# A mixture-of-experts kernel: expert rows fetched in 32-channel pieces and turned by VectorE in 32x32 squares

## The chip, the cores and the metric

The kernel runs on one core of a Trainium2 chip. The metric is the device time of one execution in microseconds. A core has five engines with queues of their own: PE (matrix multiply), DVE (VectorE), ACT (ScalarE), POOL (GpSimd) and SP (which issues most DMAs here). Engines wait for each other and for DMAs through semaphores. The profile calls PE's loading of a stationary operand PEld; it lies beside the multiplications.

## What is computed

Two layers over 2708 nodes with 256 channels. Layer 0 is a graph attention, then a causal self-attention with a mixture of experts; layer 1 is a second graph attention and a second mixture of experts. Only the mixture of experts is touched. Cut from the reference (layer 0; layer 1 has no `ln2_w`):

```python
flat = _rmsnorm(x, ln2_w).reshape(-1, Cx)
probs = jax.nn.softmax(flat @ router_w.T, axis=-1)
tp, ti = jax.lax.top_k(probs, TOPK)                       # 2 of 8 experts
tp = tp / (jnp.sum(tp, axis=-1, keepdims=True) + 1e-09)
weights = jnp.sum(tp[..., None] * jax.nn.one_hot(ti, NE, dtype=flat.dtype), axis=1)
for e in range(NE):
    hh = jax.nn.silu(flat @ w1[e].T) * (flat @ w3[e].T)   # 256 -> 682
    out = out + weights[:, e:e + 1] * (hh @ w2[e].T)      # 682 -> 256
```

Everything is in float32.

## The kernel before

The router sends each node's row, twice, into a DRAM buffer `xs`: expert `e` owns the rows from `e * CAP` on, filled from the front. A row of `xs` has 268 floats (1072 bytes): 256 channels, the node's number, eight expert weights, and filling.

Each expert has five fixed blocks of 128 rows. Some are computed already before the stage (three in layer 0, four in layer 1), and the last two of expert 7 in layer 0 later. What an expert needs beyond five blocks is done in half blocks of 64 rows of any expert, two halves at a time. `experts_blocks` (L2011) runs the rest. It makes a list `units`: for each expert its left blocks in pairs, a single one where the number is odd, and ahead of each of the experts 2 to 5 a unit of two half blocks, whose experts are read from a table at run time (`e` is None there). Both layers have 25 units. Experts 2 to 5 have a cycle of four units: halves, pair, pair, single.

For each unit:

- `fetch` (L2037) has SP load the rows of its blocks, 128 rows x 1072 bytes each (L2049, halves at L2045), into slots of `XR`, a ring of 17 slots. A slot is free again when the rows computed from it have been added to the output, since it holds the node numbers by which the addition is addressed.
- `front` (L2057) brings the channels onto the partitions: two TensorE transposes per block (L2063) of 128x128 into a PSUM tile `pt`, then ACT copies it to `xT` in SBUF (L2065 in layer 1). In layer 0 it does so in two activations which also multiply by `ln2_w` (L2068).
- `up` (L2072) has PE multiply by w1 and w3 in six groups of hidden channels (L2085), in five PSUM banks `pup` by turns; ACT applies silu (L2089), DVE the product (L2090, L2093), which gives `hT`. Half blocks go through `up_halves` (L2116 and after).
- `down` (L2096) has PE multiply by w2 (L2100), DVE weigh the rows (L2103), and POOL add them to the output in DRAM by node number (`add_rows`, L621). Half blocks: `down_halves`, L2150.

In iteration `k` of the main loop, the code issues weight loads, `fetch` of unit `k + 5` (`AHEAD`), `up` of unit `k`, `front` of unit `k + 2`, and `down` of unit `k - 1`. So on PE the transposes of unit `k + 2` stand between `up` of `k` and `down` of `k - 1`. The framework then orders each engine's instructions by their dependencies and its own estimates, so that SP's fetches and loads come in another order than they stand in the code.

Expert weights (2.1 MB an expert, six DMAs each, L2004 to L2009) go by turns into three rooms (`arena` twice, `room`), two experts ahead. The half blocks' two experts go into two further rooms, `more`, which are free again after the last product of the former halves (L2150).

Of the kernel before, what the change touches and what calls it, by code (L numbers as in the profile page):

```python
# [10 lines left out]
F32 = mybir.dt.float32  # L11
AF = mybir.ActivationFunctionType
# [8 lines left out]
P = 128  # L21
N = 2708
C = 256
KC = C // P
# [13 lines left out]
GI = 6  # L38
NB = 5
HALF_B = 64  # L40
AHEAD = 5
MORE = 8
LEAST, MOST = 512, 960
# [6 lines left out]
CAP = (NT + 1) * P  # L50
# [12 lines left out]
V_C1, V_C2, V_SS, V_SD, V_B1, V_LN1, V_LN2 = range(0, 14, 2)  # L63
# [86 lines left out]
def adj_ffn_kernel(ctx, tc, x, adj, vecs, bias_rows, tab, w_gnn0, w_gnn1, wqkv, wo,  # L150
                   r0, r1, w1_0, w3_0, w2_0, w1_1, w3_1, w2_1, out):
    nc = tc.nc
# [27 lines left out]
    vec = const.tile([P, 14], F32, name="vec")  # L180
# [434 lines left out]
    def add_rows(acc, ys, tokens, layer, e=None):  # L615

        i = nc.gpsimd.indirect_dma_start(  # L621
            out=acc[:, :], out_offset=bass.IndirectOffsetOnAxis(ap=tokens.bitcast(I32), axis=0),
            in_=ys, in_offset=None, compute_op=ALU.add,
            **(dict(bounds_check=N - 1, oob_is_err=False) if layer else {}))
        now, past = added.setdefault(acc.name, [[], []])
        if now and now[0][0] != (e, layer) or e is None:
            past[:], now[:] = now, []
        for _, name in past:
            tc.add_manual_dep(i.ins, name, NEEDS, reason="may add to the same rows")
        now.append(((e, layer), i.ins.name))  # L630
        if e is not None:
            key = f"{acc.name}_{layer}_{e}"
            tc.declare_no_dep(i.ins, group=key, reason="other tokens")
            tc.add_to_no_dep_group(key, i.ins)
# [1201 lines left out]
    def after_all(i, xs):  # L1836
        for name in written[xs.name]:
            tc.add_manual_dep(i.ins, name, NEEDS, reason="reads what they wrote")
# [132 lines left out]
    def clear(xs, e):  # L1971

        at, n = e * CAP + LEAST, MOST + HALF_B - LEAST
        nc.sync.dma_start(out=xs[at:at + n, :].rearrange("(b p) c -> p b c", p=P),
# [17 lines left out]
    def load_expert(room, w1, w3, w2, e, used=False):  # L1992
        cut = NF * P
        a, b, c, d = weights_at(room)
        if not used:
            nc.gpsimd.memset(c, 0.0)
            nc.gpsimd.memset(d[:, NF, :], 0.0)
        if isinstance(e, int):
            w1v, w3v = (w[:, e, :].rearrange("(k p) h -> p k h", p=P) for w in (w1, w3))
            w2v = w2[e]  # L2000
        else:
            w1v, w3v = (w[:, bass.ds(e, 1), :].rearrange("(k p) o h -> p k (o h)", p=P) for w in (w1, w3))
            w2v = w2[bass.ds(e, 1)].rearrange("o h c -> (o h) c")
        nc.sync.dma_start(out=a, in_=w1v[:, :, :cut])  # L2004
        nc.sync.dma_start(out=b, in_=w3v[:, :, :cut])
        nc.sync.dma_start(out=c[:, :, :REST], in_=w3v[:, :, cut:])
        nc.sync.dma_start(out=c[:, :, HIGH:], in_=w1v[:, :, cut:])
        nc.sync.dma_start(out=d[:, :NF, :], in_=w2v[:cut, :].rearrange("(k p) c -> p k c", p=P))
        nc.sync.dma_start(out=d[:REST, NF, :], in_=w2v[cut:, :])  # L2009

    def experts_blocks(layer, w1, w3, w2, xs, acc, arena):  # L2011
# [8 lines left out]
        with ExitStack() as s:  # L2020
            sp = s.enter_context(tc.tile_pool(name=f"slot{layer}", bufs=2))
# [6 lines left out]

            ring = [XR[:, t, :] for t in range(AHEAD, NT)]

            with tc.tile_pool(name=f"bpu{layer}", bufs=5, space=PSUM) as pu, \
# [4 lines left out]

                def fetch(unit):  # L2037
                    xts = []
                    for e, j in unit:
                        xt = ring.pop(0)  # L2040
                        ring.append(xt)
                        if e is None:
                            for h in range(2):
                                row = register(tab[0:1, 1, j + h:j + h + 1], NE * CAP - HALF_B)
                                after_all(nc.sync.dma_start(out=xt[h * HALF_B:(h + 1) * HALF_B, :],  # L2045
                                                            in_=xs[bass.ds(row, HALF_B), :]), xs)
                        else:
                            row = e * CAP + j * P
                            after_all(nc.sync.dma_start(out=xt, in_=xs[row:row + P, :]), xs)  # L2049
                        xts.append(xt)  # L2050
                    return xts

                def register(of, top):
                    return nc.values_load(of, engines=[SP], min_val=0, max_val=top,
                                          skip_runtime_bounds_check_because="the table is clamped")

                def front(xts):  # L2057
                    B = len(xts)
                    pt = pt_.tile([P, KC, 2, P], F32, tag="tr", name="pt")
                    xT = sp.tile([P, KC, 2, P], F32, tag="xT", name="xTs", bufs=3)  # L2060
                    for b, xt in enumerate(xts):
                        for c in range(KC):
                            nc.tensor.transpose(pt[:, c, b, :], xt[:, c * P:(c + 1) * P], ident)  # L2063
                    if layer == 1:
                        nc.scalar.copy(xT[:, :, :B, :], pt[:, :, :B, :])  # L2065
                    else:
                        for c in range(KC):
                            nc.scalar.activation(xT[:, c, :B, :], pt[:, c, :B, :], AF.Copy,  # L2068
                                                 scale=vec[:, V_LN2 + c:V_LN2 + c + 1])
                    return xT  # L2070

                def up(k, w, xT, B, between):  # L2072

                    hT = hTs[k % len(hTs)]
                    for n in range(NHC):
                        if n == NHC // 2:
                            between()
                        pp = pu.tile([P, 2, 2, P], F32, tag="pp", name="pup")
                        if n < NF:
                            parts = [(w[i][:, :, n * P:(n + 1) * P], P) for i in range(2)]  # L2080
                        else:
                            parts = [(w[2], HIGH + REST)]
                        for i, (wn, to) in enumerate(parts):
                            for c in range(KC):
                                nc.tensor.matmul(pp[:to, i, :B, :], wn[:, c, :], xT[:, c, :B, :],  # L2085
                                                 start=(c == 0), stop=(c == KC - 1))
                        sl = sp.tile([P, 2, P], F32, tag="sl", name="sl", bufs=3)
                        if n < NF:
                            nc.scalar.activation(sl[:, :B, :], pp[:, 0, :B, :], AF.Silu)  # L2089
                            nc.vector.tensor_tensor(hT[:, n, :B, :], sl[:, :B, :], pp[:, 1, :B, :], ALU.mult)  # L2090
                        else:
                            nc.scalar.activation(sl[:REST, :B, :], pp[HIGH:HIGH + REST, 0, :B, :], AF.Silu)
                            nc.vector.tensor_tensor(hT[:REST, n, :B, :], sl[:REST, :B, :], pp[:REST, 0, :B, :], ALU.mult)  # L2093
                    return hT
# [10 lines left out]

                halves = [slice(h * HALF_B, (h + 1) * HALF_B) for h in range(2)]

# [38 lines left out]
                def down_halves(w, hT, xt, gk):  # L2146
# [7 lines left out]
                    upper = sp.tile([P, 1], F32, tag="upper", name="upper")  # L2154
                    nc.vector.tensor_copy(upper[:HALF_B].bitcast(I32), xt[halves[1], C:C + 1].bitcast(I32))
                    add_rows(acc, yw[halves[0]], xt[:HALF_B, C:C + 1], layer)
# [44 lines left out]
                units = []  # L2201
                for e in range(NE):
                    left = [(e, j) for j in range(NB) if (e, j) not in done]
                    if 2 <= e < 2 + MORE // 2:
                        units.append([(None, 2 * (e - 2))])
                    units += [left[i:i + 2] for i in range(0, len(left), 2)]
                xt = [fetch(u) for u in units[:3]]
                nxt = [front(x) for x in xt[:2]]
                asked, more_asked = 1, 0
                waiting, downs = [], {}  # L2210
                for k, unit in enumerate(units):
                    e = unit[0][0]
                    if k == 1:
                        table()
                        xt += [fetch(u) for u in units[3:AHEAD + 1]]

# [5 lines left out]
                    if k == 0 or e is not None and e + 2 < NE and asked < e + 2 and units[k - 1][0][0] == e:  # L2222
                        asked += 1
                        load_expert(rooms[asked % 3], w1, w3, w2, asked, asked > 2)
                    if k and k + AHEAD < len(units):
                        xt.append(fetch(units[k + AHEAD]))
                    if unit[0] == (2, 2):
# [24 lines left out]
                    if k + 2 < len(units):  # L2252
                        nxt.append(front(xt[k + 2]))
# [159 lines left out]
```

## Time and profile before

| | us |
|---|---|
| median of 3 runs | 1482.06 |
| lowest and highest run | 1481.34, 1487.33 |
| the profiled execution | 1481.93 |
| its span, first to last instruction | 1479.8 |
| PE busy in the span | 1401.3 (95%) |
| DVE busy | 754.4 (51%) |
| ACT busy | 564.5 (38%) |
| POOL busy | 525.7 (36%) |

The span in 40 slices of 37 us, busy share in tenths (9 is 90% or more):

```profile
PE   6878999999999999999999899999999999999995
DVE  5688999975676322222222474767665322222221
ACT  2577866755544322222221454444333211222220
DMA  7689767440001476575212770624412867553111
```

The expert stage of layer 0 runs from about 503 us to 812 us (slices 14 to 22), that of layer 1 from about 1154 us to the end (slices 32 to 40). There PE is full and the other engines are mostly idle. The DMA row is the mean share of the 16 DMA engines. A busy PE alone doesn't say that PE sets the end; the chain of waits, followed back from the last instruction, does.

### The profile page before, as it was taken

The numbers are of one execution on the slowest core, as the hardware profiler recorded it, in microseconds if no ns is written. First come the engines' busy times: TensorE is split into PE (matmuls) and PEld (weight loads), VectorE is DVE, ScalarE is ACT, GpSimd is POOL, SyncE is SP. The second block draws the span as 40 slices with busy tenths as digits, with TensorE's granted clock in tenths as the row PEclk, the third lists the DMA queues.
The fourth block names the chain that finished last, engine by engine and source line by source line (L and its number), as shares of the span: only waits on it lengthen the run. The fifth ranks groups of instructions, "written<-read, shape, count | busy, mean of one in ns | idle before, by whom it ended". The sixth has DMA issues, their size and how long they took to land.

```text
span 1479.8 us, 20690 instructions
## 1 busy us (share of the span) xinstructions
PE 1401.3 (95%) x7344; PEld 1021.5 (69%) x7344; DVE 754.4 (51%) x1629; ACT 564.5 (38%) x1123; POOL 525.7 (36%) x677
## 2 busy tenths in 40 slices
PE   6878999999999999999999899999999999999995
PEld 5633433433334887888888878888768878888885
DVE  5688999975676322222222474767665322222221
ACT  2577866755544322222221454444333211222220
POOL 5677668773243312222222210031434212222222
PEclk9999999999999999999999999999999999999998
DMA  7689767440001476575212770624412867553111
GB/s 265 199 296 288 241 208 236 139 146 15 8 30 50 126 218 194 141 195 158 37 16 26 167 154 1 139 66 115 132 58 57 265 171 196 157 161 88 19 18 21
DMA packets 190679, 193.03 MB, mean 130 GB/s; under 512 B 90568, under 2 KB 162728, under 8 KB 187856
## 3 DMA queue, kind: packets, MB, share of 16 engines
q1 hardware_dynamic: 166262, 162.30, 35.5%
q0 software_dynamic: 20032, 25.71, 9.7%
q10 hardware_dynamic: 4270, 3.58, 0.7%
q8 instruction: 60, 0.98, 0.3%
q14 instruction: 55, 0.45, 0.1%
HBM read 119.81 MB, written 56.11 MB: 119 GB/s over the span
## 4 chain that ended last, share of the span: by engine, by line
PE 77%; DVE 8%; DMA 6%; POOL 4%; issue 2%; ACT 2%; another core or an unknown queue 0%; POOLq 0%; DVEq 0%; SPq 0%; ACTq 0%
PE pup L2085 23%; PE po L1602 14%; PE y L2100 12%; PE o L1146 5%; PE stt L1120 4%; DMA X<-hd,ix 3%; PE up L561 3%; PE pup L2116 3%; PE y L2150 1%; DVE es L1165 1%; DVE yT L1203 1%; PE pt L2063 1%; PE pm L1221 1%; PE po L948 1%; PE pt L584 1%
## 5 line engine op out<-in xcount | busy, mean ns | idle before, releaser
L2085 PE MATMUL pup<-xTs,arena 128*128 128x256 f32 (+2 forms) x1320 | 252.3, 350 | 0.6 <-ACT xTs L2068 0.6
L2085 PEld LDWEIGHTS pup<-xTs,arena 128*128 128x128 f32 (+1 forms) x1320 | 219.8, 190 | 27.7 <-PE y L2150 1.5
L1602 PE MATMUL po<-hb,PT 128*128 128x257 f32 (+2 forms) x968 | 226.0, 387 | 2.6 <-DVE PT L1595 2.6
L2089 ACT ACTIVATE sl<-pup 128x256 f32<-128x256 f32 (+1 forms) x210 | 73.7, 351 | 375.1 <-PE pup L2085 354.2
L1602 PEld LDWEIGHTS po<-hb,PT 128*128 128x128 f32 (+2 forms) x968 | 175.9, 188 | 41.6 <-issue 12.7
L2090 DVE TENSOR_TENSOR hT<-sl,pup 128x256 f32<-128x256 f32 (+1 forms) x210 | 79.6, 380 | 228.5 <-ACT sl L2089 228.3
L1126 ACT ACTIVATE e<-stt 128x1024 f32<-128x1024 f32 (+1 forms) x132 | 125.6, 986 | 93.0 <-PE stt L1120 63.8
L621 POOL DMA_INDIRECT out<-ys,XR x44 | 68.0, 1546 | 237.2 <-DVE ys L2103 169.2
L1165 DVE TENSOR_TENSOR es<-es,e 128x1024 f32<-128x1024 f32 x104 | 136.1, 1309 | 29.9 <-ACT e L1126 22.0
L621 POOL DMA_INDIRECT acc<-ys,XR x44 | 68.4, 1554 | 225.1 <-DVE ys L2103 153.7
L2100 PE MATMUL y<-arena,hT 128*128 128x256 f32 x612 | 136.7, 379 | 0.0
L1120 PE MATMUL stt<-qT,kT 64*128 64x512 f32 (+1 forms) x528 | 132.4, 611 | 4.3 <-ACT e L1126 3.9
L1829 POOL DMA_INDIRECT xs<-XR,place x88 | 93.3, 1061 | 91.7 <-DVE mk L1589 39.6
L1146 PE MATMUL o<-e,V 128*64 128x512 f32 (+1 forms) x528 | 124.3, 594 | 0.0
L2100 PEld LDWEIGHTS y<-arena,hT 128*128 128x128 f32 x612 | 114.3, 190 | 14.5
L1580 ACT ACTIVATE E<-sb,dcol 128x768 f32<-128x768 f32 (+1 forms) x88 | 75.3, 859 | 110.2 <-DVE PT L1595 106.7
L2103 DVE TENSOR_SCALAR ys<-y,XR 128x256 f32<-128x256 f32 x71 | 34.3, 484 | 146.6 <-PE y L2100 146.4
L2085 PE MATMUL pup<-xTs,room 128*128 128x256 f32 (+3 forms) x528 | 99.9, 346 | 0.0
L1120 PEld LDWEIGHTS stt<-qT,kT 64*128 64x128 f32 x528 | 44.4, 187 | 76.5 <-issue 62.3
L2085 PEld LDWEIGHTS pup<-xTs,room 128*128 128x128 f32 (+1 forms) x528 | 85.4, 189 | 9.8 <-PE y L2150 0.8
L1146 PEld LDWEIGHTS o<-e,V 128*64 128x64 f32 x528 | 33.0, 138 | 70.6 <-issue 55.6
L994 DVE MAX8 tops<-arena 128x8 f32<-128x2708 f32 (+1 forms) x22 | 65.3, 2970 | 0.3 <-DMA arena<-in_adj 0.3
(316 smaller groups left out, 1992.4 us busy)
## 6 DMA issues: line engine op xcount, KB each, us to landing
more<-in_w SPq DMA_DIRECT2D x48, 640.0 KB
arena<-in_adj SPq DMA_DIRECT2D x21, 1354.0 KB
arena<-in_w SPq DMA_DIRECT2D x36, 640.0 KB
mb<-mb SPq DMA_DIRECT2D x44, 352.0 KB
XR<-xs SPq DMA_DIRECT2D x80, 134.0 KB
xs<-none SPq DMA_DIRECT2D x16, 536.0 KB
room<-in_w SPq DMA_DIRECT2D x12, 640.0 KB
acc<-X SPq DMA_DIRECT2D x21, 128.0 KB
```

Of the source, the lines that this page charges most:

```text
L621: i = nc.gpsimd.indirect_dma_start(out=acc[:, :], out_offset=bass.IndirectOffsetOnAxis(ap=tokens.bitcast(I32), axis=0), in_=ys, in_offset= ...
L1120: nc.tensor.matmul(st[:r, g, c0(sb):], kT[a:b, sb * P:sb * P + r], qT[a:b, t0 + (sb == t0 + 1):t0 + 2, :, :], start=True, stop=True)
L1126: nc.scalar.activation(e[:r, :, c0(sb):], v[sb, "st"][:r, :, c0(sb):], AF.Exp, scale=1.0 / HD ** 0.5)
L1146: nc.tensor.matmul(v["o"][g * HD:(g + 1) * HD, c:], V[:r, sb, g * HD:(g + 1) * HD], v[sb][:r, g, c:], start=(n + i == 0), stop=(n + i == t ...
L1165: nc.vector.tensor_tensor(es, es, v[sb][:r, :, c:], ALU.add)
L1580: nc.scalar.activation(e[:q, :n], sb[:q, i0:i1], AF.Exp, bias=dcol[:q, j:j + 1], scale=SLOPE - 1.0)
L1602: nc.tensor.matmul(v["po", i][:r, :F], v["PT", j][:q, a:a + r], hb[:q, j, :], start=(j == 0), stop=(j == NT - 1))
L1829: i = nc.gpsimd.indirect_dma_start(out=xs[:, :], out_offset=bass.IndirectOffsetOnAxis(ap=at, axis=0), in_=src, in_offset=None)
L2085: nc.tensor.matmul(pp[:to, i, :B, :], wn[:, c, :], xT[:, c, :B, :], start=(c == 0), stop=(c == KC - 1))
L2089: nc.scalar.activation(sl[:, :B, :], pp[:, 0, :B, :], AF.Silu)
L2090: nc.vector.tensor_tensor(hT[:, n, :B, :], sl[:, :B, :], pp[:, 1, :B, :], ALU.mult)
L2100: nc.tensor.matmul(y, hT[:, n, b, :], w[3][:, n, :], start=(n == 0), stop=(n == NHC - 1))
```

## The change

For the pair and single units of fixed blocks, other than the first two of each layer (`in_pieces`), the 256 channels are no longer loaded as rows. SP loads only the last 12 floats of each row into the ring slot, and the channels in eight DMAs into a new tile `pieces`: each takes 32 channels of all rows of the unit and puts row `32 s + j` on partition `j` of one quarter of 32 partitions, at place `s`. So each of its runs is 32 floats, 128 bytes, and a pair has 256 runs in each DMA. There are five such tiles (`AHEAD`), each free again once it is turned. `front` then has DVE transpose all 32x32 squares within the tile, straight into `xT`: one instruction for a pair (128 x 512), two for a single block (128 x 128 each). In layer 0 ACT multiplies `xT` by `ln2_w` in place. Half-block units and the first two units keep the TensorE transposes. What is computed is the same.

```diff
+SQ = 32
 def fetch(unit):
     xts = []
+    in_pieces = unit[0][0] is not None and unit not in units[:2]
...
             row = e * CAP + j * P
-            after_all(nc.sync.dma_start(out=xt, in_=xs[row:row + P, :]), xs)
+            c0 = C if in_pieces else 0
+            after_all(nc.sync.dma_start(out=xt[:, c0:], in_=xs[row:row + P, c0:]), xs)
         xts.append(xt)
+    if in_pieces:
+        (e, j), B = unit[0], len(unit)
+        row = e * CAP + j * P
+        pieces = sp.tile([P, KC, 2, P], F32, tag="xp", name="pieces", bufs=AHEAD)
+        for k in range(KC):
+            for a in range(P // SQ):
+                c0 = k * P + a * SQ
+                after_all(nc.sync.dma_start(
+                    out=pieces[a * SQ:(a + 1) * SQ, k, :B, :].rearrange("j b (s i) -> j (b s) i", i=SQ),
+                    in_=xs[row:row + B * P, c0:c0 + SQ].rearrange("(s j) i -> j s i", j=SQ)), xs)
+        turned.append(pieces)
+    else:
+        turned.append(None)
     return xts
...
 def front(xts):
     B = len(xts)
+    xT = sp.tile([P, KC, 2, P], F32, tag="xT", name="xTs", bufs=3)
+    pieces = turned.pop(0)
+    if pieces is not None:
+        if B == 2:
+            nc.vector.transpose(xT.rearrange("p k b c -> p (k b c)"), pieces.rearrange("p k b c -> p (k b c)"))
+        else:
+            for c in range(KC):
+                nc.vector.transpose(xT[:, c, 0, :], pieces[:, c, 0, :])
+        if layer == 0:
+            for c in range(KC):
+                nc.scalar.activation(xT[:, c, :B, :], xT[:, c, :B, :], AF.Copy,
+                                     scale=vec[:, V_LN2 + c:V_LN2 + c + 1])
+        return xT
     pt = pt_.tile([P, KC, 2, P], F32, tag="tr", name="pt")
-    xT = sp.tile([P, KC, 2, P], F32, tag="xT", name="xTs", bufs=3)
     for b, xt in enumerate(xts):
         for c in range(KC):
             nc.tensor.transpose(pt[:, c, b, :], xt[:, c * P:(c + 1) * P], ident)
```

More of the change, by code (lines that the diff above doesn't have):

```diff
@@ L2055, in register @@
                                           skip_runtime_bounds_check_because="the table is clamped")
+                turned = []
                 def front(xts):
                     B = len(xts)
+                    xT = sp.tile([P, KC, 2, P], F32, tag="xT", name="xTs", bufs=3)
[11 more added lines that the diff above has]
+                        return xT
                     pt = pt_.tile([P, KC, 2, P], F32, tag="tr", name="pt")
-                    xT = sp.tile([P, KC, 2, P], F32, tag="xT", name="xTs", bufs=3)
                     for b, xt in enumerate(xts):
```

## The prediction

> **What bounds the kernel now.** I read the page first, then the two expert stages alone (the busy time in stretches 500 to 830 us and 1150 to 1480 us), then the chain of waits inside one expert, then the groups and SP's issues there.
>
> The stretches, with columns for the time and busy time of PE, PE's weight loads, DVE, ACT and POOL, then the granted clock, the DMA share and GB/s:
>
> ```profile
> 500.00:830.00 330.00, 325.61 (x1866) 277.64 (x1865) 83.25 (x242) 72.81 (x204) 75.23 (x62) 0.99 0.51 132
> 1150.00:1480.00 330.00, 313.13 (x1745) 265.29 (x1744) 80.09 (x242) 63.70 (x169) 70.41 (x51) 0.98 0.47 123
> ```
>
> PE is busy 98.7% and 94.9% of these stretches, DVE 25% and 24%, ACT 22% and 19%, the DMA engines about half. A busy PE is not yet a PE that ends last, so the chain of waits is what I rely on (start, length, what):
>
> ```profile
> 630.10 9.69 PE pup L2085 x44
> 639.79 0.22 PE pt L2063 x2
> 640.01 5.18 PE y L2100 x24
> 645.20 4.90 PE pup L2085 x44
> 650.10 0.44 PE pt L2063 x4
> 650.53 5.18 PE y L2100 x24
> 655.72 4.82 PE pup L2116 x40
> 660.54 0.59 PE pt L2063 x4
> 661.13 2.59 PE y L2100 x12
> ```
>
> It is PE work end to end. The transposes of `front` (L2063) stand in it with their whole length: two of them put 0.22 us between `up` and `down`, four 0.44 us, so 0.109 us each. The 0.59 us after the half-width products of L2116 holds 0.15 us more. The groups give each transpose a longer time, because a matmul's record includes its latency; the step in the chain is what counts:
>
> ```profile
> L2063 PE MATMUL pt<-ident,XR 128*128 128x128 f32 x158 | 27.0, 282 | 3.1 <-DMA XR<-xs 2.3 <-ACT xTs L2065 0.8
> L2068 ACT ACTIVATE xTs<-pt,vec 128x256 f32<-128x256 f32 (+1 forms) x50 | 18.6, 424 | 18.5 <-PE pt L2063 18.1
> L2065 ACT COPY xTs<-pt 128x512 f32<-128x512 f32 (+1 forms) x25 | 12.5, 501 | 13.8 <-PE pt L2063 9.2 <-DMA XR<-xs 4.2
> L2090 DVE TENSOR_TENSOR hT<-sl,pup 128x256 f32<-128x256 f32 (+1 forms) x210 | 79.6, 380 | 228.5 <-ACT sl L2089 228.3
> ```
>
> DVE waits 228 us for ACT at L2090 alone, ACT 354 us for PE at L2089: neither is the bound. SP is ahead of the work: it stops at row fetches until an old row slot has been added to the output, which is 17 blocks back in the ring:
>
> ```profile
> SPq L2049 <- DMA acc<-ys,XR: 86.5, 16, 12.4
> SPq L2049 <- DMA out<-ys,XR: 80.0, 17, 12.6
> ```
>
> **What the Trainium skill says.** "VectorE: DVE Perf Modes", section "The three transpose paths", gives VectorE 311 ns for a 128x128 bf16 transpose in 32x32 blocks and says that only such blocks are turned. The trace has no such instruction; as a size for it, L2090's 380 ns (shapes mixed) for mostly 256 f32 columns is of the same order. The same section warns that a copy which transposes by strides is 19 times slower when the innermost stride is large. Here the innermost run is 32 floats, contiguous at both ends, so I don't apply the factor. "DMA: Bandwidth & Descriptors", section "Why small descriptors are slow (HBM only)", names a fixed cost per packet and per descriptor. The trace agrees that small packets are poor in GB/s, and it has a near relative, the leftover weight columns (L2006 and L2007: 256 runs of 168 bytes each). In two quarter-microsecond stretches where these runs dominate:
>
> ```profile
> DMA packets 270, 0.06 MB, mean 235 GB/s; under 512 B 263, under 2 KB 263, under 8 KB 270
> q1 hardware_dynamic: 270, 0.06, 113.5%
> ...
> DMA packets 154, 0.02 MB, mean 95 GB/s; under 512 B 154, under 2 KB 154, under 8 KB 154
> q1 hardware_dynamic: 154, 0.02, 55.8%
> ```
>
> The share counts 16 engines, 4 engine-us in a quarter: 1.135 x 4 / 270 = 16.8 ns and 0.558 x 4 / 154 = 14.5 ns a packet. I take 15 ns for one of 128 bytes, bounds 10 and 30 (a read across a boundary, rows 1072 bytes apart).
>
> **The change, part by part.** A unit is one or two blocks of 128 rows. Each layer has 25 units, of which four are half-expert units and two are the first two; these six keep the old way. That leaves 19 units with 31 blocks in layer 0 and 19 with 32 in layer 1: 25 pairs and 13 singles, 63 blocks.
>
> *Removed from PE:* 63 x 2 = 126 of the 158 transposes, 126 x 0.109 = 13.7 us, all on the chain. If the extra 0.15 us after L2116 goes too (four places in layer 0 and three in layer 1), that is 1.0 us more. I take it as staying with whatever PE does next, since the switch from half-width products remains.
>
> *Added on DVE:* 25 turns of 128x512 and 26 of 128x128. From L2090 and the skill's 311 ns I estimate 0.3 us for the small one and 0.7 us for the large: 25 x 0.7 + 26 x 0.3 = 25 us in both layers together, bounds 20 and 60. DVE has 497 us free in the two stretches. In DVE's compiled order a turn stands among the hT products of the unit two before its own, and while it waits or runs, those products queue behind it. PE feels that only when all five `pup` banks are full. A group of a pair takes 9.50 / 6 = 1.6 us, so about 8 us are covered. A large turn of even 2 us leaves nothing visible. Without that cover each pair would lose its 0.7 us, 17 us in all.
>
> *ACT:* in layer 0 the scaling stays, now in place from SBUF and behind a turn; 38 activations of about 0.42 us become 38 of the same size. In layer 1, 19 copies of 0.5 us go, off the chain. Nothing counted: the up products need xT two units later, over 15 us.
>
> *DMA engines:* 63 x 1024 = 64,512 packets of 128 bytes at 15 ns are 968 engine-us, plus 8,064 row tails of 48 bytes at 13 ns, 105; less 8,064 row packets of 1072 bytes at about 55 ns (fitted over the stages' windows without software DMAs), 444. Net 629 engine-us, over 16 engines 39 us, spread over some 540 us. The share rises from about 0.5 to 0.57. Nothing on the chain.
>
> *SP:* each of the 38 units gains eight DMAs. L2006 with its 256 runs issues in 0.37 to 0.42 us, and a row fetch of L2049 in 0.36, so the issue time doesn't follow the run count. 38 x 8 x 0.45 = 137 us over both layers. In the compiled program each hardware DMA also waits for the one eight places before it, so eight are in flight at most. With 3 us each, that allows one per 0.4 us, about the issue time. In a steady expert of 46.7 us SP goes from 25 DMAs to 49. Weights that used to slip between row fetches now follow them. For expert 4, the pieces buffers (five) let its two pair fetches go at once, the half-expert weights still wait for L2150 at 582.5 us, and expert 4's own follow at about 590, ahead of the 603 us of before and of the need at 664.
>
> The tightest place is the start of layer 1: fifteen piece and tail DMAs come ahead of the half-expert weights, whose last issue was at 1176.9 us. 15 x 0.45 moves this to 1183.7, landing at about 1187 to 1188; PE wants them at 1195. Covered by 7 us; pieces of 1 us each would use it up.
>
> *Sum:* 13.7 us saved, and I allow 0.7 us for small waits at the two starts, where DMA is already 80% busy (507 to 553 us). The profiled execution took 1481.93 us (its span 1479.8), so 1481.9 - 13.0 = **1468.9 us**. The median of the three runs is 1482.06, 0.1 us off, so I use the number for it too.
>
> **Rivals.** *Part of the gain is given back (1478 us).* Late pieces at the start of a layer, or the turn standing in DVE's queue, hold PE for 4 to 5 us in each layer: 1468.9 + 2 x 4.5. For it: DMA is full there and weights are bunched with pieces. Against: the slack of 7 us above, and in layer 0 the half-expert weights are wanted only at 561 us and were all issued by 529.
>
> *Slower: SP cannot feed both (1522 us).* One mechanism, in each of the middle experts. Between one wait for L2150 and the next, 46.7 us, SP must issue 49 DMAs. The 20 weight and half-unit DMAs take about 13 us (half-expert sets cost some 0.65 us a DMA with their register loads), which leaves 34 us for 24 pieces and 5 tails. It decides from 1.2 us each. At 1.5 us an expert gets 29 x 0.3 = 9 us longer; with six experts' worth in all, 54 us, less the 13.7 gained: 1522. For it: single issues stretch to 1.8 us when weights are bunched, and the limit of eight in flight ties pieces to them. Against: it needs landings near 10 us on average, and 0.36 to 0.42 us is the rule.
>
> *The DMA engines fill up* is the same sign but farther off: 660 us x 16 x 0.51 = 5,390 free engine-us over 64,512 packets allow 83 ns a packet, five times what I measured.
>
> *That the transposes remain* is excluded by the compiled order: 32 of 158 are left.
>
> **How the numbers follow.** Forecast 0.74; its own range is 1466 (no allowance, the 0.15 us gone too) to 1473 (bounds of turn and packet costs). Partial gain 0.13, slower 0.12, 0.01 for a larger gain. To leave out no more than 2 in 10, the range goes up into the partial case: 1465 to 1479. Half a per cent, about what this kernel's measurement can tell from no change, is 7.4 us; faster means under 1474.7. Faster: 0.74 plus 0.02 of the partial case and the rest, 0.77; within: 0.11; slower: 0.12.
>
> **What would show it.** Right: L2063's successor with 32 transposes, chain steps `up` to `down` with no gap, a DVE transpose group of about 25 us, PE still 97% or more of the stage, SP's issues near 0.4 us. Wrong: PE idle before `pup` or its weight load with the turn, ACT's scaling or a weight DMA as releaser; DVE waiting on pieces; piece issues above 1 us.

## The result, and the profile after

The changed kernel takes 1466.28 us (median of 1465.13, 1465.24, 1467.31 and one run of 4412.35 us that the comparison leaves out); the kernel before took 1481.7 us on the same chip. The ratio, of the three others, is 0.9898, with a 95% interval of [0.9873, 0.9922]: about 1% faster, where 1468.9 us was forecast. The profiled execution took 1465.13 us, its span 1463.3. Two later comparisons of the same pair (below) gave 0.9929 and 0.9926, so the first one lies at the lucky end; the mean of the three is 0.9918.

The views of before, now of the kernel after. First the busy time in the two expert stretches (columns as before):

```profile
500.00:830.00 330.00, 325.36 (x1859) 277.29 (x1858) 100.60 (x298) 78.19 (x217) 80.12 (x70) 1.00 0.57 135
1150.00:1480.00 330.00, 299.86 (x1647) 253.16 (x1645) 88.80 (x263) 51.85 (x146) 68.77 (x50) 0.98 0.50 119
```

PE is as full as before in the first stretch: the work moves up, it doesn't leave holes. In the second, PE is busy 13.3 us less because the kernel now ends at 1463.3 us, earlier within the stretch. DVE has 17.4 and 8.7 us more (as a share of the stretch 30% and 27%), still far from a bound; the DMA share rose from 0.51 and 0.47 to 0.57 and 0.50.

The chain of waits inside one expert, of the kernel after (start, length, what):

```profile
635.05 0.22 PE pt L2093 x2
635.27 5.18 PE y L2130 x24
640.45 4.90 PE pup L2115 x44
645.35 5.18 PE y L2130 x24
650.54 4.82 PE pup L2146 x40
655.36 2.79 PE y L2130 x12
```

L2093 is L2063 of before, L2115 is L2085, L2130 is L2100 and L2146 is L2116. After the 44 `up` products the `y` products now follow at once: the 0.44 us of four transposes are gone. The 0.22 us that stays is that of a half-block unit, which keeps its transposes. After the half-width products (L2146) a `y` of 12 takes 2.79 us where it took 2.59: the switch did stay, now inside the `y` step, and there it costs 0.20 us where ahead of the transposes it cost 0.15.

The groups, of the kernel after (busy time, mean ns of one, idle time before them and what ended it):

```profile
L2093 PE MATMUL pt<-ident,XR 128*128 128x128 f32 x32 | 5.8, 279 | 2.5 <-DMA XR<-xs 1.6 <-ACT xTs L2095 0.8
L2081 DVE STREAM_TRANSPOSE xTs<-pieces 128x512 f32<-128x512 f32 x25 | 17.8, 711 | 5.5 <-DMA pieces<-xs 4.2
L2084 DVE STREAM_TRANSPOSE xTs<-pieces 128x128 f32<-128x128 f32 x26 | 7.2, 297 | 0.0
L2087 ACT ACTIVATE xTs<-xTs,vec 128x256 f32<-128x256 f32 (+1 forms) x38 | 16.4, 464 | 26.3 <-DVE xTs L2084 15.7 <-DVE xTs L2081 10.6
```

32 of 158 transposes are left on PE. The turns take 17.8 + 7.2 = 25.0 us of DVE, 0.71 us for a pair and 0.30 us for one half of a single block. ACT waits 26 us for turns and DVE 4.2 us for pieces, but none of this reaches PE. PE's own waits in the whole of layer 0's stage that have to do with the rows are these, of the kernel after (us in total, times, longest), and in layer 1's stage there is none:

```profile
PE pt L2093 <- DMA XR<-xs: 1.6, 1, 1.6
PE pup L2115 <- ACT xTs L2098: 0.6, 1, 0.6
```

Both belong to the first unit of the layer, which is fetched as before; before, they were 2.3 and 0.6 us. In `e9_again`, a repetition of the changed kernel, the first is 2.1 us (1.61 and 0.51), so the difference is not the change's.

### The profile page after: what moved, and what is told of

It is laid out like the page before. It is cut to its first block, busy times and chain, and to the rows that moved or that the text cites. A ratio compares the mean times of both kernels' runs of the same rounds, so it can differ in the third digit from the quotient of the medians.

```text
span 1463.3 us, 20902 instructions
## 1 busy us (share of the span) xinstructions
PE 1385.9 (95%) x7218; PEld 1006.3 (69%) x7218; DVE 775.9 (53%) x1680; ACT 555.3 (38%) x1104; POOL 525.3 (36%) x677
## 4 chain that ended last, share of the span: by engine, by line
PE 77%; DVE 8%; POOL 6%; DMA 5%; issue 2%; ACT 1%; SPq 0%; POOLq 0%; DVEq 0%; ACTq 0%
PE pup L2115 23%; PE po L1603 15%; PE y L2130 13%; PE o L1147 4%; PE stt L1121 4%; PE up L562 3%; DMA X<-hd,ix 3%; PE pup L2146 3%; PE y L2180 1%; DVE yT L1204 1%; DVE es L1166 1%; PE po L949 1%; DVE ix L999 1%; POOL ra L804 1%; DVE tops L995 1%
## 5 line engine op out<-in xcount | busy, mean ns | idle before, releaser
L2115 PE MATMUL pup<-xTs,arena 128*128 128x256 f32 (+2 forms) x1320 | 249.7, 348 | 0.6 <-ACT xTs L2098 0.6
L2115 PEld LDWEIGHTS pup<-xTs,arena 128*128 128x128 f32 (+1 forms) x1320 | 218.5, 189 | 27.2 <-PE y L2180 1.5
L1603 PEld LDWEIGHTS po<-hb,PT 128*128 128x128 f32 (+2 forms) x968 | 176.7, 189 | 42.8 <-issue 13.3
L2130 PE MATMUL y<-arena,hT 128*128 128x256 f32 x612 | 137.3, 380 | 0.0
L2130 PEld LDWEIGHTS y<-arena,hT 128*128 128x128 f32 x612 | 114.6, 190 | 19.7 <-DVE hid L2154 4.9
L2115 PE MATMUL pup<-xTs,room 128*128 128x256 f32 (+3 forms) x528 | 99.9, 346 | 0.0
L2115 PEld LDWEIGHTS pup<-xTs,room 128*128 128x128 f32 (+1 forms) x528 | 85.4, 189 | 9.8 <-PE y L2180 0.8
```

What stands on the lines that cost most here:

```text
L1603: nc.tensor.matmul(v["po", i][:r, :F], v["PT", j][:q, a:a + r], hb[:q, j, :], start=(j == 0), stop=(j == NT - 1))
L2130: nc.tensor.matmul(y, hT[:, n, b, :], w[3][:, n, :], start=(n == 0), stop=(n == NHC - 1))
```

## Where the time went

To see the gain without the rest of the program, I cut PE's timeline into stages: from the first `up` product of a layer's expert stage to its last `y` product, and what lies between the layers. Each row is one profiled execution; the clock is the mean of what was granted to PE from 503 to 530 us, as a share of full speed. The last five rows are runs of the experiments below.

| kernel | layer 0 | between | layer 1 | clock |
|---|---|---|---|---|
| before | 304.10 | 343.85 | 308.85 | 0.87 |
| after | 294.87 | 344.53 | 302.04 | 1.00 |
| after, repeated (`e1_again`) | 296.53 | 347.00 | 302.04 | 0.94 |
| after, repeated (`e9_again`) | 297.60 | 345.06 | 302.04 | 0.87 |
| `e2_idle_pe` | 301.48 | 344.90 | 308.85 | 1.00 |
| `e3_layer1` | 301.48 | 347.26 | 302.05 | 1.00 |
| `e5_turn4` | 296.56 | 345.78 | 302.04 | 0.94 |

Layer 1 repeats to 0.01 us: 308.85 - 302.04 = 6.81 us for 64 transposes, 0.1064 us each. In layer 0 the pair of profiles differs by 9.23 us, which is too much for 62 transposes. The reason is PE's clock in the 27 us around the start of the stage. In the kernel before and the kernel after:

```profile
503.00:530.00 27.00, 24.18 (x105) 20.23 (x104) 8.16 (x33) 6.64 (x17) 3.15 (x7) 0.87 0.88 279
```

```profile
503.00:530.00 27.00, 24.70 (x118) 21.18 (x117) 10.03 (x38) 7.87 (x20) 3.65 (x9) 1.00 0.56 135
```

The third column from the end is the granted clock, the next the DMA share. It is tempting to say that the lighter DMA load gave PE its clock. The table refutes that: `e9_again` is the changed kernel and has 0.87, with a DMA share of 0.56, and `e3_layer1`, which loads whole rows in layer 0, has 1.00 with a share of 0.89. The mean hides something simpler. In windows of half a microsecond the clock is either full or half, and half for one stretch: 6.8 us long in the kernel before (506.3 to 513.1 us) and in `e9_again` (507.5 to 514.3), 3.4 us in `e1_again` and `e5_turn4`, and absent in the three runs of 1.00. A stretch of 6.8 us at half speed loses 3.4 us, most of it inside the stage.

So compare runs of equal clock. At 1.00: 301.48 - 294.87 = 6.61 us for 62 transposes, 0.1066 us each. At 0.87, before against `e9_again`: 304.10 - 297.60 = 6.50 us. Both layers together: **13.4 us**, all of it PE's time for the transposes. The spans of the first pair of profiles differ by 16.5 us. Beyond the 13.4, 2.6 us of that are the clock in layer 0, and 1.8 us lie after the last `y` product (15.2 us before, 13.4 after). Ahead of layer 0's stage and between the layers the kernel after takes 1.3 us more. I put none of these down to the change: the clock varies as shown, `e3_layer1`, which has the change in layer 1, takes 15.6 us after its last `y`, and the times outside the stages vary from run to run.

## The experiments

Each edit is against the kernel after, unless it says otherwise; ratios are to the kernel before, measured on the same chip in the same session.

**The change repeated** (`e1_again` and `e9_again`, no edit). The first comparison had three runs of the changed kernel; these have six each.

> The changed kernel once more, against the kernel before on the same chip. Theory A (the gain is the time of the 126 transposes taken off PE, 0.109 us each, and nothing else): ratio 0.9908, 13.7 us under before. Theory B (some 2 to 3 us of the gain come from elsewhere, from a first stretch of layer 0 with fewer rows in flight and a higher granted clock): ratio 0.988 to 0.989, and the clock between 503 and 530 us is 1.00 again.

> The changed kernel once more, to narrow the interval. Theory A (what goes is TensorE's time of the 126 transposes, 6.8 us in layer 1 and 6.6 us in layer 0, and nothing is given back): a ratio of 0.991, 13.4 us of 1481.6. Rival B (part is given back in waits at the starts of the layers, as the first repetition with its 0.9929 could be read): 0.993 or above. Rival C (the first comparison's 0.9898 is the size of it, so that something beside the transposes was saved): 0.990 or below.

Measured: 1470.27 us, ratio 0.9929 [0.9906, 0.9952], and 1468.49 us, ratio 0.9926 [0.9906, 0.9947]. Their intervals start above the first median ratio of 0.9898, so it is likely to overstate the gain. The stage sum of 13.4 us would be 1 - 13.4 / 1481.7 = 0.9910, inside all three intervals. Whether 1 or 2 us are given back somewhere can't be decided: the time between the layers varies by 3 us from one execution to the next in the table, and nothing of the change is there.

**PE does the transposes after all, of the identity, into a bank that nobody reads** (`e2_idle_pe`). Everything else of the change stays. If the gain is PE's time, it must vanish.

```diff
                     if pieces is not None:
+                        idle = pt_.tile([P, KC, 2, P], F32, tag="tr", name="idle")
+                        for b in range(B):
+                            for c in range(KC):
+                                nc.tensor.transpose(idle[:, c, b, :], ident, ident)
```

> The changed kernel, and PE also makes the 126 transposes of the identity into a bank that nobody reads. All of DMA, SP, DVE and ACT stays as changed. Theory A: PE's time is the whole gain, so it is back at before, ratio 0.999 to 1.001. Theory B: 2 to 3 us stay gained, ratio 0.998. A third theory, that the fetch in pieces costs something which the transposes' gain hides: above before, ratio over 1.001.

Measured: 1479.37 us, ratio 0.9990 [0.9972, 1.0007]. The gain is gone. The interval alone would still allow the 2 to 3 us of theory B; the stages decide, with 301.48 us, as in `e3_layer1`, which transposes layer 0's rows on PE, and 308.85 us, to the hundredth that of before. The chain of `e2_idle_pe` shows the same gap again at the same place:

```profile
644.19 4.90 PE pup L2119 x44
649.09 0.44 PE idle L2083 x4
649.53 5.18 PE y L2134 x24
654.71 4.82 PE pup L2150 x40
659.53 0.59 PE idle L2083 x4
660.12 2.59 PE y L2134 x12
```

These steps are those of the kernel before, 0.44 and 0.59 us. What the change adds (pieces, turns, eight DMAs a unit) costs nothing here that a ratio can show; what it removes is all of the gain.

**Pieces in layer 1 alone** (`e3_layer1`).

```diff
-                    in_pieces = unit[0][0] is not None and unit not in units[:2]
+                    in_pieces = layer == 1 and unit[0][0] is not None and unit not in units[:2]
```

> Pieces and turns in layer 1 only, rows and TensorE transposes in layer 0. Theory A: 64 transposes go, 7.0 us, ratio 0.9953. Theory B: the extra lies in layer 0, so the same 7.0 us here, and the expert stage of layer 0 is as long as before, 304 us from first up to last y, with a clock under 0.9 between 503 and 530 us.

Measured: 1474.38 us, ratio 0.9957 [0.9945, 0.9968], which is 6.4 us. Layer 1 has 302.05 us, as in the full change, and layer 0 has 301.48 us, as with the transposes. The two layers add up and don't help or hinder each other.

**Each turn four times** (`e5_turn4`), to see whether turns that take longer reach PE.

```diff
+                        for _ in range(4):
-                        if B == 2:
-                            nc.vector.transpose(xT.rearrange("p k b c -> p (k b c)"), pieces.rearrange("p k b c -> p (k b c)"))
+                            if B == 2:
+                                nc.vector.transpose(xT.rearrange("p k b c -> p (k b c)"), pieces.rearrange("p k b c -> p (k b c)"))
...
```

> Every turn on DVE is made four times over: 75 large ones and 78 small ones more, 75 x 0.71 + 78 x 0.30 = 77 us of DVE, a pair's turns take 2.8 us together. Cover as forecast (five pup banks, about 8 us): as the changed kernel, ratio 0.989 to 0.993, the expert stage of layer 1 still 302.0 us. Rival (DVE's turns stand in the path of the hT products): half of it shows, some 35 us, ratio over 1.01.

Measured: 1469.23 us, ratio 0.9908 [0.9893, 0.9924], no slower than the change itself. DVE's turns, of `e5_turn4`:

```profile
L2082 DVE STREAM_TRANSPOSE xTs<-pieces 128x512 f32<-128x512 f32 x100 | 70.5, 705 | 5.1 <-DMA XR<-xs 2.2
L2085 DVE STREAM_TRANSPOSE xTs<-pieces 128x128 f32<-128x128 f32 x104 | 26.7, 289 | 1.2
```

97.2 us of turns in place of 25.0, and layer 1 still takes 302.04 us. But this is a weaker test of the cover than it looks. For most pairs the compiled order puts one turn ahead of the unit's last `hT` product and the other three behind it, DVE's timeline of `e5_turn4`:

```profile
648.77 0.71 DVE L2082 STREAM_TRANSPOSE xTs<-pieces 128x512 f32<-128x512 f32 x1
649.40 0.24 DVE L2124 TENSOR_TENSOR hT<-sl,pup 42x128 f32<-42x128 f32 x1
649.58 2.18 DVE L2082 STREAM_TRANSPOSE xTs<-pieces 128x512 f32<-128x512 f32 x3
```

The most that stands in a row ahead of an `hT` product is 1.46 us (518.23 us), and four large turns in a row, 2.94 us, stand only ahead of a half-block unit's products (561.82 us). So four times the turns cost nothing in this order; how much the five `pup` banks would cover was not tried.

**Each piece fetched twice** (`e4_twice`), the second time into a tile that nobody reads. It doubles packets and piece DMAs, to find the point at which SP or the DMA engines decide.

```diff
                         turned.append(pieces)
+                        spare = sp.tile([P, KC, 2, P], F32, tag="xq", name="spare", bufs=AHEAD)
+                        for k in range(KC):
+                            for a in range(P // SQ):
+                                c0 = k * P + a * SQ
+                                after_all(nc.sync.dma_start(
+                                    out=spare[a * SQ:(a + 1) * SQ, k, :B, :].rearrange("j b (s i) -> j (b s) i", i=SQ),
+                                    in_=xs[row:row + B * P, c0:c0 + SQ].rearrange("(s j) i -> j s i", j=SQ)), xs)
```

> Each piece is fetched twice, the second time into tiles that nobody reads: 304 DMAs and 64,512 packets of 128 bytes more, the rest as changed. Theory A with the covers as worked out (DMA engines have room for some 83 ns a packet, SP for 1.2 us an issue with 49 DMAs an expert, here 73): the same as the changed kernel within 3 us, ratio 0.989 to 0.992. Rival (SP's queue is nearly used up by eight more DMAs a unit): weights come late, PE idles before pup of the middle experts, 20 us or more, ratio over 1.003.

Measured: 1498.42 us, ratio 1.0127 [1.0102, 1.0152], and stages of 308.34 and 314.21 us, 11 to 12 us longer in each layer than the repetitions of the change. But no wait of PE for a piece or a weight shows in the stages. (Just ahead of layer 1's stage PE's second set of transposes waits 4.7 us for ACT's copy, where the kernel after waits 0.8; I did not follow that.) What changed is the compiled order on PE. In the kernel after, the 40 products of a half-block unit stand together, on PE's timeline:

```profile
604.78 4.89 PE L2146 MATMUL pup<-more,xTs 128*64 128x512 f32 x40
```

In `e4_twice` (L2153 there) they stand in three parts with `up` products between them:

```profile
611.48 2.15 PE L2153 MATMUL pup<-more,xTs 128*64 128x512 f32 x6
...
617.21 2.37 PE L2153 MATMUL pup<-more,xTs 128*64 128x512 f32 x14
...
620.13 2.73 PE L2153 MATMUL pup<-more,xTs 128*64 128x128 f32 x20
```

That is 7.25 us of work in place of 4.89. In the order of before and after, the two half experts take turns product by product; here three products of the first stand ahead of any of the second. The trace shows why that costs time. Asked for 604.70 to 605.20 us of the kernel after and for 611.40 to 611.90 us of `e4_twice`, the timeline has:

```profile
604.78 0.65 PE L2146 MATMUL pup<-more,xTs 128*64 128x512 f32 x2
```

```profile
611.48 0.64 PE L2153 MATMUL pup<-more,xTs 128*64 128x512 f32 x1
```

In the first, two products of 512 columns, one of each half expert, start 0.01 us apart, and the next two 0.48 us later. In the second, one starts alone, and the next, again alone, 0.48 us later. So a product without its partner takes the time of a pair. Four such units in each layer are 4 x 2.36 = 9.4 us of the 11 to 12. So this run tests the framework's order and not, as meant, SP, and leaves its question to the next one.

**The same, with the half-block products held by turns** (`e7_twice_kept`: `e4_twice`, and each of these products depends, for the order alone, on the one before it).

```diff
+KEPT = mybir.DependencyInfo(mybir.DependencyClass.NoSync, mybir.DependencyReason.DATA)
...
+                                if before_this is not None:
+                                    tc.add_manual_dep(m.ins, before_this, KEPT, reason="the halves by turns")
+                                before_this = m.ins.name
```

> The doubled fetch of before, with the half-expert products held in their by-turns order. If their broken order (7.0 us a unit in place of 4.8, eight units) is what made the doubled fetch slow, most of the 28 us go: ratio 0.993 to 1.000. If SP's 49.9 us an expert binds, PE now waits for weights: ratio 1.008 or more, with waits of PE on more, arena or room.

Measured: 1494.22 us, ratio 1.0087 [1.0071, 1.0104]; layer 0 takes 313.40 us, layer 1 304.01. Now PE does wait, of `e7_twice_kept` from 505 to 820 us:

```profile
PE pup L2155 <- DMA more<-in_w: 8.8, 4, 3.9
```

It is not a piece that comes late but a half expert's weights, which stand behind the pieces in SP's queue. Layer 0 is 16.9 us longer than in `e1_again`, which has the same clock at the start. Besides the 8.8 us of waits, the clock is half for 3.4 us after each of the two longest waits (3.92 and 2.74 us; not after that of 1.86), which loses 3.4 us. And in each of the four units two half-block products are still split off ahead of the others, about 1 us each (as in `e8_wider_kept` below). That is 16.2 us. In layer 1 no product is split off and the stage is 2.0 us longer than the change's; 1.3 us of that is slower first `up` products, and 0.5 us a wait for another part of the program.

In the kernel after, SP still has a gap in every expert. SP's timeline of the kernel after:

```profile
610.25 0.41 SPq L2005 DMA_DIRECT2D more<-in_w  x1
...
612.61 0.37 SPq L2008 DMA_DIRECT2D more<-in_w  x1
624.95 0.37 SPq L2009 DMA_DIRECT2D more<-in_w  x1
...
637.40 6.99 SPq L2061 DMA_DIRECT2D pieces<-xs  x8
...
647.79 4.16 SPq L2061 DMA_DIRECT2D pieces<-xs  x8
...
653.01 4.54 SPq L2061 DMA_DIRECT2D pieces<-xs  x8
658.13 0.41 SPq L2005 DMA_DIRECT2D more<-in_w  x1
```

From one expert's first half-expert weight to the next it is 47.88 us, and between 612.98 and 624.95 us SP waits 11.97 us for the former half blocks' last product, a wait that it could lose. So the 49 DMAs of an expert need 35.9 us, 0.73 us each. In `e7_twice_kept` the same distance is 51.5 us without a gap:

```profile
601.74 0.41 SPq L2006 DMA_DIRECT2D more<-in_w  x1
...
653.21 0.41 SPq L2006 DMA_DIRECT2D more<-in_w  x1
```

73 DMAs in 51.5 us are 0.71 us each, and PE needs only 45.7 us for an expert (1302.93 to 1348.61 us in the chain of the kernel after). So SP's queue, its waits for earlier DMAs included, is the bound of `e7_twice_kept` in layer 0. While PE waits longest, the DMA engines are full too (share 1.10 from 659.0 to 664.2 us), so part of SP's time is that of transfers it waits for. An estimate from 0.71 us and 45.7 us is that about 64 DMAs an expert would be the most that SP feeds. In layer 1 SP's distance is as long (1294.08 to 1344.78 us), but PE waits for no weight; my reading, which no run tests, is that the layer is over before the lead that SP has is used up.

**Each piece DMA cut in two** (`e6_halved`): twice the DMAs, the same packets. It is to part SP's issue work from the DMA engines'.

```diff
+                                for h in range(2):
+                                    n = B * P // 2
+                                    part = pieces[a * SQ:(a + 1) * SQ, k, h, :] if B == 2 else pieces[a * SQ:(a + 1) * SQ, k, 0, h * n:(h + 1) * n]
...
+                                        in_=xs[row + h * n:row + (h + 1) * n, c0:c0 + SQ].rearrange("(s j) i -> j s i", j=SQ)), xs)
```

> Each piece DMA is cut into two of half as many runs: 304 DMAs more, packets and bytes as in the changed kernel. If SP's issuing was what made the doubled fetch slow: as slow as that or nearly, ratio 1.005 to 1.013. If the doubled packets on the DMA engines did it: as the changed kernel, 0.990 to 0.993. If only the order in which the half-expert products were compiled did it: in between, by as much as the products of L2146's kind take longer than 4.8 us a unit.

Measured: 1486.78 us, ratio 1.0036 [1.0023, 1.0049]. SP again has no gap, and from one expert to the next it needs 50.1 us (597.89 to 648.01), as much as with double packets (49.9 in `e4_twice`, 601.06 to 650.94), so between these two runs it is the number of DMAs that counts and not that of packets. As in `e4_twice` the compiled order of the half-block products is another, which mixes a second cost into the ratio, so only SP's distance is read from this run.

**Half-block units in pieces too** (`e8_wider_kept`), with the second unit of each layer, and the products held as above.

```diff
-                    in_pieces = unit[0][0] is not None and unit not in units[:2]
+                    in_pieces = unit is not units[0]
...
+                                at = slice(h * HALF_B, (h + 1) * HALF_B)
+                                after_all(nc.sync.dma_start(out=xt[at, C:], in_=xs[bass.ds(row, HALF_B), C:]), xs)
+                                for k in range(KC):
+                                    for a in range(P // SQ):
...
```

> The half-block units and the second unit of each layer go through pieces and turns too, half-expert products held by turns: 24 more transposes leave PE, 2.6 us. SP issues 73 more DMAs an expert's cycle less 8, 65 in 46 us. If SP still keeps up: 2.6 us under the changed kernel, ratio 0.988 to 0.991 where the changed kernel stands near 0.991. If SP is used up: slower than the changed kernel, over 0.994.

Measured: 1473.97 us, ratio 0.9941 [0.9921, 0.9961], not better than the change, though PE has fewer transposes. SP's gap is gone here as well, and the first two half-block products are split off, in the chain of `e8_wider_kept`:

```profile
653.46 1.00 PE pup L2158 x2
654.46 2.79 PE y L2141 x12
657.25 4.82 PE pup L2158 x36
```

5.82 us for these products where the change has 4.82: the two that are split off start one after the other (653.39 and 653.87 us) and not as a pair, which costs 1.00 us, more than the two transposes of the unit saved (0.22 us). The ratio is where the rival (SP used up) put it, but PE waits for no piece and no weight in either stage, so the rival's path is not shown.

**The second unit of each layer in pieces, no half blocks** (`e11_second`), with one more piece tile. Eight more transposes leave PE.

```diff
-                    in_pieces = unit[0][0] is not None and unit not in units[:2]
+                    in_pieces = unit[0][0] is not None and unit is not units[0]
...
-                        pieces = sp.tile([P, KC, 2, P], F32, tag="xp", name="pieces", bufs=AHEAD)
+                        pieces = sp.tile([P, KC, 2, P], F32, tag="xp", name="pieces", bufs=AHEAD + 1)
```

> The changed kernel with the second half-block pair of each layer also fetched in pieces, so that 8 more transposes leave TensorE, with one more piece tile. Theory A: they are worth 8 x 0.1065 = 0.85 us, if their pieces land in time: the stage of layer 1 comes down from 302.04 to 301.6 us, and the ratio to 0.6 thousandths below that of the changed kernel beside it. Rival B (the start of a layer is where DMA is latest): the pieces come late, TensorE waits before the second pair's first product for some microseconds, and the stage of layer 1 or of layer 0 is longer than without, by 1 to 5 us.

Measured: 1465.87 us, ratio 0.9908 [0.9886, 0.9929], beside 0.9926 for the change in the same session. Layer 1 took 304.51 us and not 301.6, which by the letter is what the rival expected. PE's timeline says something else. In `e9_again`, from the router's last product to the end of the first `up` products of layer 1:

```profile
1149.24 0.36 PE L2227 MATMUL y<-hsum,allones 128*128 128x8 f32 x2 [0.67 <-DVE ys L589]
1149.46 0.64 PE L2093 MATMUL pt<-ident,XR 128*128 128x128 f32 x4
1150.89 0.65 PE L2093 MATMUL pt<-ident,XR 128*128 128x128 f32 x4 [0.80 <-ACT xTs L2095]
1151.38 19.16 PE L2115 MATMUL pup<-xTs,arena 128*128 128x256 f32 x88
```

and in `e11_second`:

```profile
1143.60 0.36 PE L2227 MATMUL y<-hsum,allones 128*128 128x8 f32 x2 [0.67 <-DVE ys L589]
1143.81 0.63 PE L2093 MATMUL pt<-ident,XR 128*128 128x128 f32 x4
1145.24 20.95 PE L2115 MATMUL pup<-xTs,arena 128*128 128x256 f32 x88 [0.80 <-ACT xTs L2095]
```

The four transposes stood ahead of the first `up` product, outside the stage as I had cut it: from the router's product to the first `up` it is 1.64 us in place of 2.14, a gain of 0.50 us. The same 88 products then took 1.79 us longer, without a wait among them, because the granted clock was 0.66 for five microseconds, of `e11_second`:

```profile
1145.00:1150.00 5.00, 4.76 (x14) 3.91 (x15) 2.63 (x17) 0.57 (x2) 2.10 (x7) 0.66 0.67 85
```

In `e9_again` the corresponding stretch had 1.00. The other 0.7 us of layer 1 lie in its first half-block products, 5.51 us in place of 4.82; the profile names no wait there, and the cause is open. So neither theory's number for the stage was right: PE waits for no piece, and the saving is there, but elsewhere. The execution as a whole is shorter because the time between the layers is 339.89 us, 5 less than in `e9_again`, of which the edit explains the 0.50. Whether the kernel as a whole is faster than the change stays undecided, since the intervals overlap by far.

**The general network run always** (`e10_both`), to see whether the one run of 4412 us was one in which the flag of the tuned network was raised and the general one ran after it.

```diff
-    with tc.If(again > 0):
+    with tc.If(again > -1):
```

> The changed kernel with the general network run always, after the tuned one, by the test of its flag against -1 in place of 0. If the one execution of 4412 us was a run in which the flag was up and both networks ran, this one takes 4412 us within 1%. If it was a stall of another kind, this one takes another time, and that execution stays without a cause.

Measured: 4224.92 us (one run), 4.2% less than that execution, which is outside the 1% I had set. The size is near, the time isn't the same, and the execution never came again in the runs of these experiments. Its cause stays open.

## Why the prediction was right

- *Removed from PE.* 126 x 0.109 = 13.7 us was forecast; the runs show 6.81 + 6.61 = 13.4 us, 0.1065 us a transpose. The term is 2% off, and the 0.05 us by which the switch from half-width products grew accounts for that: eight places (four in layer 1 too, where the forecast counted three) are 0.4 us. The mechanism is shown twice: the gain goes when PE gets idle transposes back (`e2_idle_pe`), and half of it goes with half of the change (`e3_layer1`). The trace's own duration of 279 ns a transpose would have given 35 us; taking the step in the chain was what made the number right. That the switch would stay is also borne out.
- *Added on DVE.* Forecast 25 us from 0.7 and 0.3 us a turn; measured 25.0 us from 0.71 and 0.30. "VectorE: DVE Perf Modes", section "The three transpose paths", of the Trainium skill gives 311 ns for a 128x128 bf16 turn; the trace has 297 ns for float32 of that size, so it served. The page's warning of a copy 19 times slower than the transposing DMA was left aside since the runs are 128 bytes long; nothing in the runs speaks against that. That the turns cost PE nothing is shown, even four times over (`e5_turn4`). The reason given, 8 us of cover by the `pup` banks, is not: the compiled order puts most turns just ahead of a unit's last `hT` product or behind it, so the cover was hardly put to use.
- *ACT.* Nothing was counted, and nothing shows: its 26 us of waits for turns end before PE asks.
- *DMA engines.* Forecast share 0.57, up by 0.07; measured 0.57 in layer 0's stretch and 0.50 in layer 1's, up by 0.06 and 0.03. The term was put too high, without effect.
- *SP.* Here the forecast was right for a reason that was too favourable. It took 0.45 us for a piece DMA, which is the mean issue time in the trace (448 ns). But an issue is not all that a DMA costs SP: with the waits between issues it is 0.73 us per DMA in the kernel after. The room was 11.97 us in the expert shown. The rival "SP cannot feed both" has the right mechanism and the right victim, as `e7_twice_kept` shows; it put the point of decision at 1.2 us for each of the 29 DMAs for rows. Counted in DMAs it lies, by the estimate above, at about 64 an expert, where the change has 49. So the room was there, but for SP it was 12 us and not the 20 or so that the forecast's own terms leave (46.7 less 13 and 29 x 0.45).
- *The tightest place, the start of layer 1.* PE has no wait in that stage for pieces, turns or weights. The last of the first half experts' weights was issued by 1177.0 us, 29.2 us after the stage's first product, where it had been 21.1. That is a shift of 8.1 us where 6.8 was forecast, and PE asked for them 10 us later, so the term was sound. The allowance of 0.7 us for the two starts was not needed.
- *The sum.* With the measured terms it is 1481.9 - 13.4 = 1468.5 us against the forecast of 1468.9, and medians of 1466.28, 1470.27 and 1468.49 us. That it agrees to 0.4 us is in part luck: the unneeded 0.7 us more than made up for the 0.3 us by which the gain fell short, and medians of one kernel lie up to 4 us apart. The rival of a partial gain back (1478 us) lies above the upper ends of all three intervals (1478 / 1481.7 = 0.9975).

## What to carry over

Price an operation on a full engine by the step it adds to the chain, not by its own duration in the trace, and check a gain by giving the engine its idle work back: that one run said more than all repetitions. When DMAs are cut up, count them per cycle against the issuing queue, waits between issues included, and look at whose transfers stand behind them; PE never waited for a piece, but for the weights behind them. When an edit changes what the framework sees, compare the compiled order on the bound engine before reading the time as the edit's own. And compare stages at equal granted clock, read in windows short enough to show it.

## What was not expected of the hardware

- PE's granted clock at the start of an expert stage differs from one execution to the next of the same kernel: a mean of 1.00, 0.94 and 0.87 from 503 to 530 us in three profiles of the changed kernel. In half-microsecond windows that is no half-clock stretch, one of 3.4 us, or one of 6.8 us; the stretch at the start of layer 1 in `e11_second` and the two after waits in `e7_twice_kept` are 3.4 us long too. At the start of layer 0 this is worth up to 2.7 us (294.87 to 297.60), a fifth of the gain studied. It didn't follow the DMA load (1.00 at a share of 0.89). What sets it off is open: in `e7_twice_kept` it followed PE's two longest waits, but at the start of layer 0 it came or stayed away after much the same waits.
- Half-width products of two experts by turns start in pairs 0.01 us apart, and a pair takes the step of one: 40 take 4.82 us, and about 7.1 in the order of `e4_twice` (7.25 on the timeline), where some have no partner. The difference is that of over twenty transposes.
- SP's time for a DMA did not depend on the number of runs: 73 DMAs an expert took 50.1 us with the packets of the change (`e6_halved`, half the runs in each piece DMA) and 49.9 and 51.5 us with the pieces' packets doubled (`e4_twice`, `e7_twice_kept`).
